# A transformer block on one core: first loads on two queues, bias product behind the first projections, and a new written order

## The chip, the cores and the metric

The kernel runs on one core of a Trainium2 chip. The core has five engines that work side by side: TensorE (PE, matrix products; its weight loads are listed apart as PEld), VectorE (DVE), ScalarE (ACT), GpSimd (POOL) and SyncE (SP, which here only issues DMAs). Each takes its instructions from its own queue, in the queue's order; they wait for one another by semaphores. The metric is the device time in microseconds (us) of one launch. Before the change the median of three runs is 478.84 us (478.42 to 479.89). About 0.3%, which is 1.4 us, is what a measurement of this kernel can tell from no change.

## What is computed

The input is 16 batches of 512 tokens with 256 features, in float32. The reference, cut to what matters:

```python
q, k, v = (heads(x @ W.T + b) for W, b in (Wq, bq), (Wk, bk), (Wv, bv))   # 16 heads of 16
qk_, kk_ = exp(q - max(q, -1)), exp(k - max(k, -1))
kv    = einsum('bhsd,bhse->bhde', kk_, v)
denom = einsum('bhqd,bhd->bhq', qk_, sum(kk_, 2)) + 1e-6
y     = einsum('bhqd,bhde->bhqe', qk_, kv) / denom[..., None]
x1  = layernorm(x + merge(y) @ Wo.T + bo)
h   = relu(x1 @ T(W1).T + b1)            # 1024 wide; T(W) = clip(round(W / (mean|W| + 1e-5)), -1, 1)
out = layernorm(x1 + h @ T(W2).T + b2)
```

Attention is linear: no product of tokens with tokens is formed. The two weight matrices of the feed-forward part become ternary.

## The kernel before

**Steps and the written order.** The whole program is a list of named steps. Some run once (`startup_steps`, L469 to L636: loading the weights, splitting them, making them ternary); the others run for each batch (`steps(b)`, L642 to L1230). A step is one instruction or a few on one engine: `qk3` of batch 1, for instance, is the six products that make q and k of the fourth 128 tokens of batch 1. A table `ORDER` (L103 on) gives each step a position, one number for each batch; the loop at the end (L1240 to L1251) emits the steps by these numbers and ties every instruction to the one ahead of it on its engine. So the table *is* the queue of each engine, across batches: several batches are under way at a time, and what stands first in a queue is waited for by all that stands behind it. No scheduler changes that order.

A second table, `OTHER` (L53 on), names for some steps the batches in which they run on the other of two engines. `engine()` (L407) reads it. Subtracting the maxima (`mxs`, L748), for example, is a POOL step unless the batch is listed, and then it is a DVE step; copying the upper half of the hidden values (`hc`, L1180/1182) is ACT's unless listed, and then DVE's.

**Precision.** A float32 operand is split into an upper part rounded to a faster format (a copy on ACT) and a lower part, the rest (a subtraction on DVE or POOL); a product is then three products (`TERMS`). Batch 0 goes without for q and k: its products (`qkF`, L718) use the loaded weights and tokens as they are, in plain float32, in two passes each.

**The stages of a batch.** Tokens transposed come from memory (`ldt`, L660, SP's queue; batch 0 in two halves a and b of each of two feature chunks 0 and 1), are split (`xt` L675, `xtl` L679), and multiplied with the weights of q and k (`qk` L728, or `qkF` L718). The bias is added (`mxa` L738, DVE), the maximum of each head found (`mxb` L744, DVE) and subtracted (`mxs` L748), and the exponential taken (`ex` L759/761, ACT). Sums over tokens (`ks` L782/784, `ksh` L789, `ksl` L793, product `pks` L806) give the denominators (`dena` L810, `denb` L825, `denc` L830, all DVE), and q is divided by them (`nrm` L838). In parallel the tokens, loaded again untransposed (`ldx`, L688), are multiplied with k (`g` L861, `gF` L857), then with the weights of v (`kv` L888), masked (`kvm`, `kvp`, `kvh`, `kvl`, L894 to L909) and multiplied with those of the output (`m` L916). Turned q (`qt` steps, L946 to L1012; `qtbl` is the lower part, L981) times m gives the attention's output (`o` L1134). The residual and the sum (`or`, `zr`, L1040, DVE), means, squares and variances (`nm`/`nq`/`nv`, `ym`/`yq`/`yv`, L1053 to L1086) and the scaling (`na`, `ya`, L1099 to L1105) are the two layer norms; `xb` (L871) and `x1b` (L1149) add biases ahead of them. Between them come eight hidden products for each batch (`f` L1168), their relu (`ha` L1174, ACT), upper and lower parts (`hc`, `hb` L1186, DVE), and eight products back (`z` L1205). `st` (L1224) stores.

**Accumulators.** PSUM, where products land, is divided into four tags of two banks each: one for q, k and transposes (`pbqk` uses it too), one for hidden products (`ph`; batch 0 also puts qkF2 and qkF3 there), one for the results `z` (and warm-up products), one for the rest. A product that needs a bank waits until the bank's last user has been read.

**The start.** `warm0` (L486) issues nine products of ones with ones, whose result nobody reads, and `warm1` two more much later (`WARM`, L51). `lqk0` and `lqk1` (L491 to L499) load the upper and the lower 128 rows of the weights of q and of k, four DMAs of 128 KB, all from ACT's queue. ACT then makes a tiny copy, for which it loads its table. `wh` and `wl` split these weights for the later batches. `lbqk` (L517) loads the two biases into row 0 of a tile that is zero elsewhere, and `pbqk` (L522) multiplies that tile with ones, so that the biases stand in all 128 rows; `bqke` (L526, ACT) copies them out of PSUM, and `mxa` adds them.

```python
                for j, w in enumerate((wqT, wkT)):
                    nc.scalar.dma_start(out=loaded[c][:, j * E:(j + 1) * E],
                                        in_=w[c * P:(c + 1) * P, :])
                if len(loaded) == EC:
                    nc.scalar.copy(tab, ones[:, 0:1])
```

TensorE's order at the start is: nine warm-up products, `pbqk`, `qkF0_0`, `qkF0_1` (first 128 tokens, feature chunks 0 and 1), `qkF1_0` and so on to `qkF3_1`, then `qk3` of batch 1, `warm1`, `tot0` (the sum for the ternary scale), `qk2` of batch 1, `pks` of batch 0, `gF`. SP's queue before starts with the two biases, then `ldt0a`, the tokens of batch 1, `ldt1a`, and pieces of the feed-forward weights among them. From `f0` of batch 0 on, hidden products and the next batches' q and k take turns.

Of the kernel before, what the change touches and what calls it, by code (L numbers as in the profile page):

```python
# [25 lines left out]
P = 128  # L26
# [24 lines left out]
WARM = (9, 2)  # L51
GROUPS = {"s": 2, ("y", 15): 4, ("s", 15): 4}
OTHER = {  # L53
    "mxs0": (0, 1, 6),
    "wol": (0,),
    "ks": (0, 1, 5, 8, 9, 10, 12, 15),
    "ksl": (0, 1, 2, 5, 6, 7, 9, 11, 12, 14, 15),
    "bvm": (0,),
    "kvp": (0, 3, 4, 5, 7, 9, 10, 12, 13, 15),
    "kvl": (0, 1, 3, 4, 6, 7, 8, 9, 10, 11, 12, 13, 15),  # L60
    "nrm0": (0, 7, 11, 13, 14),
    "xb0": (0, 2, 4, 5, 10, 11, 13),
    "xb1": (0, 3, 6, 10),
    "nm0": (0, 1, 2, 3, 5, 6, 10, 11, 14),
    "qc0": (0,),
    "qc2": (0,),
    "na2": (0, 3, 4, 8, 11, 12),
    "x1b1": (0, 13),
    "mxs3": (2, 6, 10, 11, 13),
    "nrm1": (2, 7, 8, 9, 10, 14),  # L70
    "ek0": (2, 3, 4, 5, 9, 10, 11, 13, 14, 15),
    "nv0": (1, 2, 4, 5, 7, 9, 10, 12, 13, 15),
    "x1b0": (0, 3, 8, 12),
    "hc1": (0, 4, 5, 6, 8, 14),
    "na0": (1, 6, 11, 13, 14, 15),
    "ek1": (3, 4, 6, 7, 8, 10, 11, 12),
    "xsl0": (3, 4, 11, 13),
    "xt1bl0": (1, 2, 4, 5, 9, 10, 13, 14),
    "hc2": (1, 6, 7, 9, 12, 14),
    "xtl1": (5, 8, 11, 12, 14),  # L80
    "hc0": (1, 3, 4, 9, 10, 11),
    "na3": (2, 4, 5, 10, 11, 15),
    "ya2": (0, 1, 5),
    "xsl1": (4, 9),
    "qtbl0": (3, 5, 7, 11, 13),
    "xtl0": (6,),
    "ym0": (1, 5, 6, 8, 9, 10, 11),
    "mxs1": (5, 7, 10, 15),
    "hc4": (2, 10, 14),
    "yv0": (1, 3, 7, 8),  # L90
    "hc5": (2, 6, 8, 9, 12, 15),
    "ya1": (1, 10, 11, 12, 13, 14),
    "qtbl1": (4, 7, 14, 15),
    "xt1bl1": (4, 5, 10, 12, 13, 14),
    "ya3": (3, 5, 11, 12, 13, 14),
    "na1": (6, 7, 14),
    "ya0": (4, 6, 8, 13, 14),
    "hc3": (7, 15),
    "hc6": (7, 12, 14, 15),
    "hc7": (9, 14),  # L100
    "yv1": (15,),
}
ORDER = {  # L103
    "lqk0": (0,),
    "lqk1": (1,),
    "wh0": (2,),
    "warm0": (3,),
    "lbqk": (4,),
    "wh1": (5,),
    "wl1": (6,),  # L110
    "ldt0a": (7, 0, 0, 0, 0, 0, 0, 0, 0, 0, 0, 0, 0, 0, 0, 0),
    "wl0": (8,),
    "pbqk": (9,),
    "bqke": (10,),
    "ldt1": (0, 11, 72, 132, 281, 334, 349, 553, 535, 734, 909, 1095, 1250, 1398, 1534, 1728),
    "ldt1a": (12, 0, 0, 0, 0, 0, 0, 0, 0, 0, 0, 0, 0, 0, 0, 0),
    "xt1": (0, 13, 74, 151, 282, 342, 499, 669, 767, 803, 1027, 1181, 1275, 1415, 1684, 1768),
    "xtl1": (0, 14, 90, 202, 317, 426, 528, 687, 834, 960, 1045, 1266, 1295, 1449, 1736, 1769),
    "ldt0": (0, 15, 81, 128, 204, 178, 416, 612, 703, 758, 864, 1194, 1272, 1410, 1492, 1511),
    "qkF0_0": (16, 0, 0, 0, 0, 0, 0, 0, 0, 0, 0, 0, 0, 0, 0, 0),  # L120
    "xt0": (0, 17, 82, 129, 297, 356, 505, 694, 779, 826, 1115, 1195, 1399, 1411, 1541, 1796),
    "xtl0": (0, 18, 91, 164, 298, 395, 515, 695, 832, 827, 1116, 1255, 1413, 1442, 1567, 1798),
    "qkF0_1": (19, 0, 0, 0, 0, 0, 0, 0, 0, 0, 0, 0, 0, 0, 0, 0),
    "mxa0": (20, 124, 189, 318, 344, 566, 654, 751, 989, 1166, 1223, 1338, 1463, 1611, 1824, 2057),
    "mxb0": (21, 126, 215, 319, 354, 592, 671, 761, 990, 1170, 1284, 1339, 1476, 1641, 1825, 2075),
    "qkF1_0": (22, 0, 0, 0, 0, 0, 0, 0, 0, 0, 0, 0, 0, 0, 0, 0),
    "mxs0": (23, 127, 233, 320, 425, 594, 672, 816, 1034, 1178, 1285, 1436, 1478, 1688, 1854, 2093),
    "qkF1_1": (24, 0, 0, 0, 0, 0, 0, 0, 0, 0, 0, 0, 0, 0, 0, 0),
    "lw1_0": (25,),
    "mxa1": (26, 98, 184, 235, 358, 485, 653, 743, 882, 1068, 1235, 1432, 1484, 1699, 1862, 1893),  # L130
    "mxb1": (27, 112, 221, 238, 360, 487, 661, 797, 899, 1129, 1236, 1433, 1485, 1718, 1872, 1962),
    "lwo": (28,),
    "woh": (29,),
    "wol": (30,),
    "ldt0b": (31, 0, 0, 0, 0, 0, 0, 0, 0, 0, 0, 0, 0, 0, 0, 0),
    "lw0_0": (32,),
    "sa0_0": (33,),
    "sg0_0": (34,),
    "exF0": (35, 141, 0, 0, 0, 0, 0, 0, 0, 0, 0, 0, 0, 0, 0, 0),
    "ldt1b": (36, 0, 0, 0, 0, 0, 0, 0, 0, 0, 0, 0, 0, 0, 0, 0),  # L140
    "qkF2_0": (37, 0, 0, 0, 0, 0, 0, 0, 0, 0, 0, 0, 0, 0, 0, 0),
    "qkF2_1": (38, 0, 0, 0, 0, 0, 0, 0, 0, 0, 0, 0, 0, 0, 0, 0),
    "qkF3_0": (39, 0, 0, 0, 0, 0, 0, 0, 0, 0, 0, 0, 0, 0, 0, 0),
    "mxa2": (40, 80, 175, 237, 440, 568, 623, 840, 945, 1035, 1292, 1312, 1571, 1661, 1802, 1990),
    "mxb2": (41, 121, 187, 289, 441, 569, 650, 842, 992, 1052, 1314, 1361, 1572, 1662, 1804, 1991),
    "lw0_2": (42,),
    "sa0_2": (43,),
    "lw0_1": (44,),
    "sa0_1": (45,),
    "qkF3_1": (46, 0, 0, 0, 0, 0, 0, 0, 0, 0, 0, 0, 0, 0, 0, 0),  # L150
    "mxa3": (47, 63, 222, 299, 389, 608, 730, 770, 922, 1064, 1202, 1359, 1532, 1664, 1751, 2004),
    "mxb3": (48, 71, 223, 307, 411, 609, 731, 777, 996, 1096, 1203, 1386, 1565, 1705, 1842, 2008),
    "mxs1": (49, 125, 225, 276, 486, 580, 686, 867, 916, 1152, 1276, 1444, 1488, 1719, 1873, 2058),
    "exF1": (50, 140, 0, 0, 0, 0, 0, 0, 0, 0, 0, 0, 0, 0, 0, 0),
    "lbo": (51,),
    "lw0_3": (52,),
    "lw1_3": (53,),
    "sa0_3": (54,),
    "sr0": (55,),
    "mxs2": (56, 122, 203, 290, 474, 578, 685, 892, 1024, 1136, 1317, 1382, 1573, 1673, 1814, 2028),  # L160
    "ldx": (57, 162, 145, 186, 418, 546, 670, 886, 934, 1107, 1335, 1401, 1568, 1619, 1764, 1972),
    "lbv": (58,),
    "sa1_0": (59,),
    "mxs3": (60, 111, 230, 326, 483, 621, 741, 820, 1022, 1145, 1282, 1456, 1570, 1716, 1895, 2070),
    "sg0_3": (61,),
    "qk3": (0, 62, 211, 262, 388, 577, 715, 766, 889, 1055, 1161, 1331, 1480, 1606, 1737, 1994),
    "lw1_1": (64,),
    "warm1": (65,),
    "tot0": (66,),
    "qk2": (0, 67, 155, 236, 392, 457, 593, 774, 884, 1018, 1190, 1302, 1495, 1634, 1793, 1915),  # L170
    "half0": (68,),
    "exF2": (69, 139, 0, 0, 0, 0, 0, 0, 0, 0, 0, 0, 0, 0, 0, 0),
    "exF3": (70, 120, 0, 0, 0, 0, 0, 0, 0, 0, 0, 0, 0, 0, 0, 0),
    "qz0": (73,),
    "ks": (75, 142, 248, 369, 502, 626, 762, 905, 1067, 1186, 1333, 1477, 1590, 1752, 1912, 2095),
    "ksh": (76, 148, 254, 370, 506, 632, 763, 917, 1075, 1192, 1371, 1481, 1600, 1753, 1913, 2119),
    "gF0": (77, 163, 0, 0, 0, 0, 0, 0, 0, 0, 0, 0, 0, 0, 0, 0),
    "qz3": (78,),
    "sg0_2": (79,),
    "sg1_0": (83,),  # L180
    "qz2": (84,),
    "ksl": (85, 149, 255, 378, 507, 633, 765, 918, 1082, 1193, 1372, 1482, 1605, 1765, 1936, 2127),
    "pks": (86, 160, 256, 390, 523, 699, 782, 941, 1106, 1217, 1387, 1497, 1620, 1777, 1937, 2136),
    "dena": (87, 161, 257, 391, 524, 700, 784, 950, 1117, 1227, 1390, 1498, 1621, 1778, 1940, 2137),
    "bvm": (88,),
    "kvb": (89, 196, 329, 406, 549, 717, 788, 987, 1150, 1218, 1427, 1506, 1632, 1783, 1945, 2159),
    "denb": (92, 177, 263, 394, 525, 701, 793, 951, 1118, 1228, 1391, 1500, 1622, 1780, 1941, 2138),
    "denc": (93, 179, 264, 398, 532, 702, 794, 952, 1119, 1240, 1404, 1525, 1638, 1792, 1942, 2139),
    "sa1_1": (94,),
    "gF1": (95, 170, 0, 0, 0, 0, 0, 0, 0, 0, 0, 0, 0, 0, 0, 0),  # L190
    "ge": (96, 171, 293, 424, 557, 668, 809, 962, 1163, 1279, 1425, 1569, 1675, 1781, 1971, 2142),
    "qk1": (0, 97, 183, 224, 357, 452, 618, 714, 862, 1046, 1234, 1403, 1457, 1695, 1819, 1892),
    "lwv": (99,),
    "kv": (100, 194, 310, 432, 562, 712, 825, 974, 1175, 1297, 1448, 1574, 1697, 1809, 1974, 2163),
    "kvm": (101, 200, 328, 433, 563, 724, 829, 976, 1177, 1298, 1462, 1582, 1706, 1810, 1975, 2169),
    "lw1_2": (102,),
    "sa1_2": (103,),
    "sg1_2": (104,),
    "lb2": (105,),
    "qk0": (0, 106, 188, 296, 337, 565, 643, 749, 968, 1165, 1206, 1316, 1452, 1610, 1800, 2037),  # L200
    "sa1_3": (107,),
    "sr1": (108,),
    "lb1": (109,),
# [185 lines left out]
def block_kernel(ctx: ExitStack, tc: tile.TileContext, x, xT, wqT, wkT, wvT, woT,  # L389
                 bq, bk, bv, bo, w1T, b1, w2T, b2, out):  # L390
    nc = tc.nc
    NB, S, E = x.shape
# [73 lines left out]
    loaded = {}  # L466
# [830 lines left out]
```

## Time and profile before

| quantity | before |
|---|---|
| median of 3 runs | 478.84 us (478.42 to 479.89) |
| profiled execution, its own time | 478.84 us |
| its span in the trace | 477.1 us |
| PE busy | 465.9 us (98%), 2964 products |
| PE weight loads, beside PE | 395.5 us (83%) |
| DVE busy | 435.0 us (91%), 855 instructions |
| ACT busy | 398.8 us (84%), 914 instructions |
| POOL busy | 369.4 us (77%), 382 instructions |
| DMA | 58.53 MB, 123 GB/s on average |

The profiled execution's own time is the median, and 1.74 us of it lie outside the span. Busy shares are averages over the whole span, over stages with different limits. A view by windows gives the busy time of each engine in a stretch of the span; the view of waits gives, for each engine, the instruction that it waited for; the timeline gives instructions in order of time, with the idle time ahead of them and what ended it in brackets.

### The profile page before, as it was taken

The page shows a single profiled execution, that of the slowest core. Times are in us where ns is not written, and L with a number is a line of the kernel's source. Part 1 is how long each engine was busy: PE and PEld are TensorE (multiplying, and loading weights), DVE is VectorE, ACT ScalarE, POOL GpSimd, SP SyncE. Part 2 cuts the span into 40 slices and gives each one's busy share as a digit, 9 for nine tenths or more (in the row PEclk, how much of TensorE's full clock was granted, in tenths as well). Part 3 has the DMA queues.
Part 4 walks back from the last instruction along what each step waited for, and adds up shares of the span by engine and source line. Part 5 has one row for each costly group of instructions (what it writes and reads, how often), then busy time and mean ns, then how long its engine had stood idle before and what let it go on. Part 6 is the DMA issues. An engine that isn't in the chain of part 4 may idle for free. (4 is left out here: it accounts for less than half of the span.)

```text
span 477.1 us, 8950 instructions
## 1 busy us (share of the span) xinstructions
PE 465.9 (98%) x2964; PEld 395.5 (83%) x2964; DVE 435.0 (91%) x855; ACT 398.8 (84%) x914; POOL 369.4 (77%) x382
## 2 busy tenths in 40 slices
PE   9999999999999999999999999999999999999994
PEld 5777888797897888889888887978888898988874
DVE  4999899999999999999999999899999799988965
ACT  4996787897969889999969899987987988988873
POOL 4679887988888979798698989989889866436432
PEclk9999999999999999999999999999999999999999
DMA  8921035261533462433544525343441154123102
GB/s 254 340 69 45 1 125 162 77 211 68 155 110 99 145 197 94 152 113 111 176 111 133 174 94 166 123 132 112 137 162 58 42 200 137 64 89 133 45 1 89
DMA packets 35667, 58.53 MB, mean 123 GB/s; under 512 B 4130, under 2 KB 21796, under 8 KB 35620
## 3 DMA queue, kind: packets, MB, share of 16 engines
q1 hardware_dynamic: 35044, 57.43, 36.8%
q10 hardware_dynamic: 576, 0.52, 0.4%
q8 instruction: 23, 0.38, 0.4%
q14 instruction: 24, 0.20, 0.1%
HBM read 34.87 MB, written 23.07 MB: 121 GB/s over the span
## 5 line engine op out<-in xcount | busy, mean ns | idle before, releaser
L1174 ACT ACTIVATE ph<-ph,b_sb 128x512 f32<-128x512 f32 x128 | 83.7, 655 | 21.5 <-PE ph L1168 20.8
L748 POOL TENSOR_TENSOR qk<-qk,mx 128x512 f32<-128x512 f32 x52 | 57.4, 1111 | 8.4 <-DVE mx L744 7.7
L759 ACT ACTIVATE ex<-qk 128x512 f32<-128x512 f32 x64 | 39.9, 626 | 10.3 <-POOL qk L748 7.5
L738 DVE TENSOR_TENSOR qk<-pqk,bqk 128x512 f32<-128x512 f32 x64 | 43.3, 680 | 2.6 <-ACT xt_1h L675 1.0
L744 DVE TENSOR_REDUCE mx<-qk 128x32 f32<-128x512 f32 x64 | 43.2, 678 | 0.9
L1149 POOL TENSOR_TENSOR x1b<-x,b_bc 128x512 f32<-128x512 f32 x26 | 34.2, 1319 | 1.5 <-ACT x L1103 1.4
L1065 ACT ACTIVATE junk_z<-x1b,nm_z 128x256 f32<-128x256 f32 x62 | 31.1, 503 | 3.5 <-POOL nm_z L1055 3.0
L1065 ACT ACTIVATE junk_o<-x,nm_o 128x256 f32<-128x256 f32 x64 | 32.0, 502 | 2.4 <-POOL nm_o L1055 2.1
L1168 PEld LDWEIGHTS <-w1f 128*128 128x128 f16 x256 | 15.7, 98 | 19.7 <-issue 16.5
L871 POOL TENSOR_TENSOR x<-x,bo_bc 128x512 f32<-128x512 f32 x21 | 29.8, 1419 | 0.6
L838 POOL TENSOR_TENSOR qs<-ex,rden 128x512 f32<-128x512 f32 x21 | 24.3, 1170 | 7.2 <-DVE rden L830 7.1
L1103 ACT ACTIVATE x<-x,nmr_o,rstd_o 128x256 f32<-128x256 f32 x43 | 24.3, 597 | 4.5 <-POOL nmr_o L1086 4.5
L1040 DVE SCALAR_TENSOR_TENSOR x<-po,x 128x256 f32<-128x256 f32 x64 | 24.5, 417 | 2.4 <-PE po L1134 1.5
L1103 ACT ACTIVATE x1b<-x1b,nmr_z,rstd_z 128x256 f32<-128x256 f32 x41 | 23.3, 597 | 3.8 <-POOL nmr_z L1086 3.7
L1040 DVE SCALAR_TENSOR_TENSOR x1b<-pz,x1b 128x256 f32<-128x256 f32 x62 | 23.4, 414 | 1.7 <-PE pz L1205 1.5
L1084 POOL TENSOR_TENSOR rstd_o<-var_o,expo 128x4 f32<-128x4 f32 x16 | 17.6, 1101 | 7.7 <-ACT var_o L1078 7.3
L825 DVE TENSOR_REDUCE den<-dent 128x64 f32<-128x1088 f32 x16 | 20.5, 1284 | 0.4
L1084 POOL TENSOR_TENSOR rstd_z<-var_z,expo 128x4 f32<-128x4 f32 (+1 forms) x19 | 19.0, 998 | 1.5 <-ACT var_z L1078 0.9
L946 DVE STREAM_TRANSPOSE rqT<-qs 128x1024 f32<-128x1024 f32 x14 | 17.4, 1241 | 2.2 <-POOL qT_10l L981 1.2
L810 DVE TENSOR_TENSOR dent<-ex,pks 128x1024 f32<-128x1024 f32 x16 | 19.3, 1208 | 0.0
L946 DVE STREAM_TRANSPOSE rx1T<-x 128x1024 f32<-128x1024 f32 x14 | 17.4, 1242 | 1.3 <-ACT x L1103 0.7
L888 PEld LDWEIGHTS pkv<-g,wv 128*128 128x128 f32 x128 | 16.2, 191 | 0.9 <-ACT g L880 0.2
(877 smaller groups left out, 2038.0 us busy)
## 6 DMA issues: line engine op xcount, KB each, us to landing
x<-in_x_dram SPq DMA_DIRECT2D x16, 512.0 KB, 4.5
xt<-in_xT_dram SPq DMA_DIRECT2D x30, 256.0 KB, 3.8
out_dram<-x1b SPq DMA_DIRECT2D x30, 256.0 KB, 2.2
wqT<-rqT SPq DMA_DIRECT2D x14, 512.0 KB, 2.9
dqT<-wqT SPq DMA_DIRECT2D x56, 128.0 KB, 2.9
wx1T<-rx1T SPq DMA_DIRECT2D x14, 512.0 KB, 2.9
dx1T<-wx1T SPq DMA_DIRECT2D x56, 128.0 KB, 3.1
w<-in_w2T_dram SPq DMA_DIRECT2D x4, 256.0 KB, 5.2
```

The costliest lines, as they stand in the source:

```text
L738: nc.vector.tensor_tensor(s.qk[t].rearrange("p g d -> p (g d)"), s.pqk[t], bqk, ALU.add)
L744: nc.vector.tensor_reduce(s.mx[t], s.qk[t], AX.X, ALU.max)
L748: engine(f"mxs{t}", b, nc.gpsimd, nc.vector).tensor_tensor(s.qk[t], s.qk[t], s.mx[t].unsqueeze(2).to_broadcast([P, 2 * NH, HD]), ALU.subtract)
L759: nc.scalar.activation(s.ex[:, t, :], qk, AF.Exp)
L871: engine(f"xb{h}", b, nc.gpsimd, nc.vector).tensor_tensor(r, r, bo_bc.unsqueeze(1).to_broadcast([P, 2, E]), ALU.add)
L946: nc.vector.transpose(pts["r"].rearrange("p (j y w) -> p j y w", j=P // SQ, w=SQ), getattr(s, src).rearrange("p t (c j v) -> p j (t c) v", ...
L1040: nc.vector.scalar_tensor_tensor(out=r, in0=p[t], scalar=1.0, in1=r, op0=ALU.mult, op1=ALU.add, accum_out=stat("sum")[:, t:t + 1])
L1065: nc.scalar.activation(junk, getattr(s, what)[:, t, :], AF.Square, bias=n.nm[:, t:t + 1], accum_out=stat("sq")[:, t:t + 1])
L1084: nc.gpsimd.tensor_tensor(stat("rstd")[:, sl], n.var[:, sl], expo[:, sl], ALU.pow)
L1103: nc.scalar.activation(r, r, AF.Identity, bias=nmr, scale=rstd)
L1149: engine(f"x1b{h}", b, nc.gpsimd, nc.vector).tensor_tensor(s.x1b[:, tt, :], s.x32[:, tt, :], b2_bc.unsqueeze(1).to_broadcast([P, 2, E]), A ...
L1174: nc.scalar.activation(s.ph[f], s.ph[f], AF.Relu, bias=b1_sb[:, f:f + 1])
```

## The change

Four edits.

The loads of the weights of q stay on ACT's queue; those of k go to SP's. The second warm-up step issues one product where it issued two. Both tables are written anew, so that the order of steps on every engine changes throughout the program, and so does the engine of many steps. At the start, the first tokens of batch 0 (`ldt0a`, `ldt1a`) now stand in front of all other loads of SP's queue, with the two halves of k's weights between and behind them, the biases next, then batch 1's tokens; and `pbqk` and `bqke` stand behind `qkF0_0` and `qkF0_1`. TensorE then goes on with `qkF2_0`, `qkF1_0`, `qkF1_1`, `qkF2_1`, `qkF3_0`, `qkF3_1`, `qk3` of batch 1, `tot0`, `qk2`, `gF0`, `pks`.

In `OTHER`, the net count of steps for each engine moves like this. DVE gains `hc` (5), `qtbl` (7), `kvl` (4), `mxs` (3), `nrm` (3), `xtl` (3), `xb` (1) and `x1b` (1), and gives up `ek` (2), `ks` (1), `ksl` (3), `xsl` (1) and `ya` (5). POOL has 19 steps fewer, ACT 4 more. SP issues the two loads of k's weights in addition.

The diff, cut to the edit of the code, the lines of the start, and some of the steps named in the prediction:

```diff
-WARM = (9, 2)
+WARM = (9, 1)
...
-    "mxs0": (0, 1, 6),
+    "mxs1": (1, 3, 10, 12, 13, 15),
+    "mxs0": (1, 2, 9, 14),
+    "mxs2": (6, 13),
+    "mxs3": (6, 9, 10),
-    "mxs3": (2, 6, 10, 11, 13),
-    "mxs1": (5, 7, 10, 15),
-    "qtbl0": (3, 5, 7, 11, 13),
-    "qtbl1": (4, 7, 14, 15),
+    "qtbl1": (2, 3, 6, 7, 10, 12, 13, 14, 15),
+    "qtbl0": (3, 6, 7, 9, 10, 12, 15),
...
-    "lqk0": (0,),
-    "lqk1": (1,),
-    "wh0": (2,),
-    "warm0": (3,),
+    "ldt0a": (0, 0, 0, 0, 0, 0, 0, 0, 0, 0, 0, 0, 0, 0, 0, 0),
+    "lqk0": (1,),
+    "ldt1a": (2, 0, 0, 0, 0, 0, 0, 0, 0, 0, 0, 0, 0, 0, 0, 0),
+    "lqk1": (3,),
     "lbqk": (4,),
-    "ldt0a": (7, 0, 0, 0, 0, 0, 0, 0, 0, 0, 0, 0, 0, 0, 0, 0),
-    "pbqk": (9,),
-    "bqke": (10,),
-    "ldt1a": (12, 0, 0, 0, 0, 0, 0, 0, 0, 0, 0, 0, 0, 0, 0, 0),
-    "qkF0_0": (16, 0, 0, 0, 0, 0, 0, 0, 0, 0, 0, 0, 0, 0, 0, 0),
-    "qkF0_1": (19, 0, 0, 0, 0, 0, 0, 0, 0, 0, 0, 0, 0, 0, 0, 0),
-    "mxa0": (20, 124, 189, 318, 344, 566, 654, 751, 989, 1166, 1223, 1338, 1463, 1611, 1824, 2057),
+    "wh0": (5,),
+    "warm0": (6,),
+    "qkF0_0": (11, 0, 0, 0, 0, 0, 0, 0, 0, 0, 0, 0, 0, 0, 0, 0),
+    "qkF0_1": (14, 0, 0, 0, 0, 0, 0, 0, 0, 0, 0, 0, 0, 0, 0, 0),
+    "pbqk": (15,),
+    "ldt0b": (16, 0, 0, 0, 0, 0, 0, 0, 0, 0, 0, 0, 0, 0, 0, 0),
+    "qkF2_0": (17, 0, 0, 0, 0, 0, 0, 0, 0, 0, 0, 0, 0, 0, 0, 0),
+    "bqke": (18,),
+    "mxa0": (24, 130, 173, 340, 376, 561, 651, 761, 950, 1167, 1191, 1350, 1457, 1579, 1809, 2042),
-    "warm1": (65,),
...
-                for j, w in enumerate((wqT, wkT)):
-                    nc.scalar.dma_start(out=loaded[c][:, j * E:(j + 1) * E],
-                                        in_=w[c * P:(c + 1) * P, :])
+                for j, (w, queue) in enumerate(((wqT, nc.scalar), (wkT, nc.sync))):
+                    queue.dma_start(out=loaded[c][:, j * E:(j + 1) * E],
+                                    in_=w[c * P:(c + 1) * P, :])
```

The two loads of `lqk0` thus go out one on each queue, and those of `lqk1` likewise. In the changed file every line behind the tables stands three lines further down.

## The prediction

> **What bounds the kernel now.** I read the page's busy times first, then the windows, the waits of PE, and the timeline of the first and last 20 us.
>
> ```profile
> span 477.1 us, 8950 instructions
> PE 465.9 (98%) x2964; PEld 395.5 (83%) x2964; DVE 435.0 (91%) x855; ACT 398.8 (84%) x914; POOL 369.4 (77%) x382
> ```
>
> PE is the bound, and DVE is close behind. From the windows (columns: us; busy us of PE, PEld, DVE, ACT, POOL; granted clock; DMA share; GB/s):
>
> ```profile
> 0.00:20.00 20.00, 18.88 (x63) 12.16 (x63) 12.53 (x25) 12.85 (x28) 9.54 (x17) 1.00 0.89 290
> 20.00:40.00 20.00, 19.06 (x95) 15.91 (x96) 19.48 (x36) 16.91 (x41) 16.21 (x17) 1.00 0.30 106
> 80.00:100.00 20.00, 20.00 (x122) 16.26 (x121) 19.47 (x36) 17.88 (x43) 18.47 (x21) 1.00 0.26 94
> 340.00:360.00 20.00, 18.77 (x116) 15.81 (x115) 19.20 (x35) 18.21 (x41) 17.38 (x17) 1.00 0.42 132
> ```
>
> The first 20 us belong to DMA (share 0.89), the next to DVE (19.48 against PE's 19.06), the middle to PE with DVE close enough to take over in bursts. The waits of PE, in us:
>
> ```profile
> PE ph L1168 <- DVE h_1l L1186: 1.7, 2, 1.2
> PE po L1134 <- DVE m_10l L931: 0.6, 1, 0.6
> PE pqT L989 <- DVE qs L838: 0.5, 1, 0.5
> PE pks L806 <- POOL ksd_0l L793: 0.4, 1, 0.4
> ```
>
> In the middle it is nearly always DVE that PE waits for. To count this, I added up PE's products at the interval from one issue to the next where nothing is waited for: 458.0 us. PE's place in time less the work done by then is 1.4 us at `qk3` of batch 1 (13.9 us), 5.5 at `f0` of batch 0 (45.5) and 12.5 at `f0` of batch 15 (454.8). So of the 12.5 us lost, 1.1 go before PE can start, about 4.1 between 14 and 45 us, and 7.0 in the middle. Longer waits in the middle, as such gaps, sum to 3.9 us (1.38 and 0.60 for h_1l, 0.78 for m_10l, 0.48 for POOL's ksd, 0.34 for `mxa`, 0.32 for h_2l).
>
> **The start, up to the first accumulator.** From the timeline:
>
> ```profile
> 1.10 4.21 PE L486 MATMUL pwarm<-ones 128*128 128x128 f32 x18 [1.10 <-DVE ones L447]
> 5.10 1.92 PE L522 MATMUL pbqk<-bqk,ones 128*128 128x512 f32 x2
> 6.81 3.77 PE L718 MATMUL pqk<-w32qk,xt 128*128 128x512 f32 x8
> 7.05 0.59 ACT L526 COPY bqk<-pbqk 128x512 f32<-128x512 f32 x1 [0.45 <-PE pbqk L522]
> 8.96 0.69 DVE L738 TENSOR_TENSOR qk<-pqk,bqk 128x512 f32<-128x512 f32 x1 [1.03 <-ACT xt_1h L675]
> ```
>
> Warm-up products hold PE until 5.10 in both kernels, so data that land earlier than that gain nothing. Then come three steps: the bias's two passes at half clock (0.85 each, to 6.81), and `qkF0_0` (0.60 + 0.43) and `qkF0_1` (0.43 + 0.43) to 8.70. After the change the same three steps stand in the order `qkF0_0`, `qkF0_1`, bias: whichever is first pays the half clock, and all are done at 5.10 + 1.71 + 1.03 + 0.86 = 8.70 again. Condition: the half token tile and q's and k's upper rows (384 KB) by 5.10 and the next 384 KB by 6.81. Before, 384 KB had landed by 3.79 and 512 KB by 5.91; SP's first DMA was issued at 1.62 behind a memset of the bias tile, and now needn't wait for that. I take no stall (bounds 0 to 0.8).
>
> The split of queues itself removes two issues from ACT (0.45 each) and adds two on SP; ACT's table load starts earlier, and both lie beside the warm-ups. PE waits for none of them: 0.
>
> What does come later is the bias: its copy ends at about 9.5 instead of 7.64, so `mxa0` starts near 9.6 instead of 8.96, +0.6 for DVE. PE covers this, as `qkF2_0` and `qkF1_0` have banks of their own (the latter takes `pbqk`'s). POOL's chain (`mxs`, 1.11 each by the page) then brings the last exponential to about 18.0 and `ks` to 18.05, which was 17.98; `pks` follows at 20.4, as before. The second warm-up product dropped is two passes of 0.11: −0.2.
>
> The granted clock is 0.5 until 7.16 in this trace, 6.06 us after the first product. [...]
>
> **20 to 46 us.** DVE has no gap to speak of from 14.6 to 47.8, and PE waits for it. From `dena` of batch 0 (20.96) to the second lower part of x1T (ends 45.28) before takes 24.32. The steps that the changed order puts in DVE's queue between these two, each at the median of its row, sum to 24.45; with the idle time that the old stretch has (24.32 less 23.45 busy, 0.9) and a subtraction that DVE did in 1.21 there, not in its mean of 0.81, 46.4 is the changed end, against 45.28. That is +1.2 (bounds: 0, if no idle remains, and +2.0 with the late bias's 0.6 and a late `qs` like the one in the waits on top).
>
> **The middle.** The costs of the engine moves, by DVE's rows:
>
> | moved to DVE | each us | sum |
> |---|---|---|
> | hc +5 (L1182) | .68 | 3.4 |
> | qtbl +7 (L981) | .9 | 6.3 |
> | mxs +3 (L748) | .81 | 2.4 |
> | nrm +3 (L838) | .83 | 2.5 |
> | xtl +3 (L679) | 1.0 | 3.0 |
> | kvl +4, xb +1, x1b +1 | .43, .85, .71 | 3.3 |
> | off: ek 2, ks 1, ksl 3, xsl 1, ya 5 | .73, 1.28, .76, 1.0, .46 | −8.4 |
>
> The sum is +12.5 us for DVE: 435.0 to about 447 of 477, 94%. (`kvl`'s rows on DVE, L909, lie at .41 to .44, those of `qtbl` at .68 to 1.35.) By the same sum over rows POOL loses some 18 us and ACT gains 1.5, and neither is the bound. On average DVE still fits. What matters is where it doesn't: I summed DVE's and PE's rows along both written orders, in pieces of 20 us of PE's work. In the old order one pair of neighbours exceeds PE: 300 to 340, DVE 44.4 against PE 41.1, excess 3.3, and there the loss grew by 3.2 (8.9 to 12.1). In the new order that pair falls to 41.5 against 39.6 (excess 1.9), but three more arise: 60 to 80 (21.6 against 20.1, 1.5), 160 to 180 (23.4 against 19.9, 3.5), 220 to 240 (22.7 against 19.9, 2.8). Together 9.7. Each has neighbours in which DVE has 2 to 4 us to spare, where before had its excess twice running. If none costs anything, before's 3.3 is gained: −3.3. If all do, 9.7 − 3.3 = +6.4. I take half, 4.85 − 3.3 = **+1.5**.
>
> **The tail.** The last `z7`, its residual, statistics, scaling and store are on the same engines in the same order; the last batch's one mean that changes engine (`ym1` to ACT) and its variance (`yv1` to POOL) are single instructions of 0.2: 0 (±0.3).
>
> **The sum**, against the profiled execution's own 478.84 us, which is also the median: 478.84 − 0.2 + 0 + 1.2 + 1.5 + 0 = **481.3 us**.
>
> [...] DMA's share is 0.81 to 1.10 of its engines from 2 to 23 us, so more queues find no free engine. [...]
>
> **The rivals.**
>
> *Faster (the other side).* The middle's bursts fall into slack: 16 batches interleave, the orders have cushions of several us between DVE's steps and PE's, and the old order's bad pair is halved. Then the middle gives −3.3 and the start only the late bias's 0.6: 478.84 − 0.2 + 0.6 − 3.3 = 475.9. It decides if PE's waits for DVE behind 60 us sum to less than 1.5 us. For it: the long waits of before are six, and none need recur. Against: DVE at 94%.
>
> *No change.* The new bursts cost what the old pair did, and idle time in DVE's first 45 us goes: 478.84 − 0.2 + 0.2 = 478.8.
>
> *The bursts cost in full.* +6.4 in the middle and +2.0 at the start: 478.84 − 0.2 + 2.0 + 6.4 = 487.0. Against it: the trace's windows before 300 us hold DVE at 19.5 of 20 with PE at 20.00 (80 to 100).
>
> *The change doesn't do what it says.* The early tokens bring nothing at PE, as reckoned above. This is in the forecast already; only if the first products wait for k's weights, now behind the first tokens on SP's queue, does it cost, up to the 0.8.
>
> **How the numbers follow.** Forecast, 480.3 to 486.0: 0.50. In full, above 486: 0.05. No change, 477.4 to 480.3: 0.17. Faster: 0.28, about a third of it below 475.5. A measurement of this kernel tells about 0.3% (1.4 us) from no change. So slower 0.55, same 0.17, faster 0.28. The range 475.5 to 486.0 leaves out 0.05 and 0.10, and takes in most of the bounds of the middle; forecasts of both signs being likely, the forecast's own range is 480.3 to 486.0.
>
> **What would show it.** In the changed profile: `qkF0_0` at 5.1 and three steps done at 8.7; `mxa0` near 9.6; the second lower part of x1T at 46.4, where PE's loss is 7 us and not 5.5; DVE busy near 447; windows near 165 to 185 and 225 to 245 with PE below 20.00 and DVE above 19.5. It is wrong if PE begins `qkF0_0` late for loads, if `f0` comes at or before 45.5, or if PE's loss in the middle is below 7.0.

## The result and the profile after

The changed kernel takes 480.44 us (median of ten runs, 479.75 to 481.19) against 478.75 us for the kernel before in the same job: a ratio of 1.0035, 95% interval 1.0025 to 1.0044, so 1.7 us more (1.2 to 2.1). The forecast was 481.3 us, in a range from 480.3 to 486.0.

The page after, its first lines:

```profile
span 478.6 us, 8946 instructions
PE 465.2 (97%) x2962; PEld 394.4 (82%) x2962; DVE 443.0 (93%) x869; ACT 400.4 (84%) x918; POOL 351.8 (73%) x364
```

DVE has 8.0 us more to do and POOL 17.6 less; PE is as busy as it was. The windows after (columns as in the prediction), the four shown there and the one in which most is lost:

```profile
0.00:20.00 20.00, 17.35 (x59) 11.03 (x59) 12.17 (x24) 12.72 (x27) 9.05 (x17) 1.00 0.87 288
20.00:40.00 20.00, 19.51 (x95) 15.80 (x96) 19.79 (x40) 17.29 (x41) 13.42 (x13) 1.00 0.35 121
60.00:80.00 20.00, 17.93 (x117) 15.48 (x116) 19.84 (x27) 13.97 (x29) 16.82 (x14) 1.00 0.42 130
80.00:100.00 20.00, 19.82 (x122) 16.27 (x121) 18.84 (x42) 17.61 (x43) 17.34 (x20) 1.00 0.32 109
340.00:360.00 20.00, 20.00 (x131) 16.80 (x130) 19.18 (x35) 18.26 (x41) 17.38 (x19) 1.00 0.41 126
```

From 60 to 80 us PE has lost 2 us beside a DVE that is busy all the time but has finished only 27 instructions, where in the other windows behind 20 us it finished 35 to 42; four of the 27 took much longer than their kind does elsewhere (two of them are named below). From 340 to 360, where the kernel before lost 1.2, nothing is lost. The waits of PE after:

```profile
PE ph L1171 <- DVE h_5l L1189: 2.2, 2, 1.2
...
PE pqk L721 <- DMA xt<-in_xT_dram: 1.1, 1, 1.1
PE pz L1208 <- DVE h_7l L1189: 1.1, 1, 1.1
PE ph L1171 <- DVE h_4l L1189: 0.6, 1, 0.6
```

Before's long waits are gone or smaller (the product behind m_10l still waits, 0.37 us at 316.54 and not 0.78), and others of the same kind are there. As the gap over PE's usual issue interval they are 1.24 us at 11.48 (tokens), 1.16 at 65.73 (h_5l), 1.23 at 78.88 (h_7l), 1.41 at 245.0 (h_5l) and 0.73 at 378.69 (h_4l). Behind the first hidden product each kernel has six gaps of more than 0.3 us; they sum to 3.9 us in before and 5.2 in after. PE's loss, counted as in the prediction, is 5.56 us at the first hidden product of batch 0 (before 5.51), and 14.41 at that of batch 15 (before 12.48). So between these two places the change costs 1.9 us, and ahead of them nothing in these two profiles, in which the full clock came at different moments (4.88 us in after, 7.16 in before).

What the slow stretch is made of shows in the timeline of PE, DVE and POOL, 76 to 79 us:

```profile
78.88 0.39 PE L1208 MATMUL pz<-w,h_7l 128*128 128x256 f32 x1 [1.07 <-DVE h_7l L1189]
```

```profile
76.46 1.76 DVE L984 TENSOR_TENSOR qT_2l<-dqT,qT_2h 128x512 fp32r<-128x512 f32 x1
78.15 0.68 DVE L1189 TENSOR_TENSOR h_7l<-ph,h_7h 128x512 fp32r<-128x512 f32 x1
```

```profile
76.38 1.29 POOL L984 TENSOR_TENSOR qT_2l<-dqT,qT_2h 128x512 fp32r<-128x512 f32 x1
77.63 1.73 POOL L785 TENSOR_TENSOR ks<-ex 128x512 f32<-128x512 f32 x1
```

DVE's first line is a subtraction that takes 0.68 us in most places. Here it takes 1.76: it ends 0.55 us after POOL's instruction that began 0.08 earlier. `h_7l`, for which PE waits, stands behind it. POOL's next takes 1.73 in its turn instead of 1.29. In before 22 DVE instructions are stretched by over 0.25 us, in after 21. Each of them reads only from SBUF and begins while a POOL instruction is under way, or within 20 ns of its start; each ends 0.15 to 0.55 us after POOL's has. The converse holds too: of DVE's additions, subtractions and products of two operands in SBUF, none that began with no POOL instruction under way, or only one of 4 columns, is stretched (68 in before, 92 in after). The four long waits of after stand behind such instructions: `qz7` (1.85, usually 0.74), `qtbl1` of batch 2 (1.76), `kvp` of batch 8 (1.13, usually 0.42) with `ya3` of batch 5 (0.89, usually 0.40), and `na2` of batch 12 (1.17, usually 0.40). `qtbl1` and `kvp` have two inputs, `ya3` and `na2` are `tensor_scalar` with one tensor: both kinds are stretched. By what means POOL's instruction does it no run shows.

### The profile page after: what moved, and what is told of

Same layout as the page of the kernel before. It is cut to its first block, busy times and chain, and to the rows that moved or that the text cites. A ratio compares the mean times of both kernels' runs of the same rounds, so it can differ in the third digit from the quotient of the medians.

```text
span 478.6 us, 8946 instructions
## 1 busy us (share of the span) xinstructions
PE 465.2 (97%) x2962; PEld 394.4 (82%) x2962; DVE 443.0 (93%) x869; ACT 400.4 (84%) x918; POOL 351.8 (73%) x364
## 5 line engine op out<-in xcount | busy, mean ns | idle before, releaser
L751 POOL TENSOR_TENSOR qk<-qk,mx 128x512 f32<-128x512 f32 x49 | 56.0, 1147 | 14.6 <-DVE mx L747 8.1
L1152 POOL TENSOR_TENSOR x1b<-x,b_bc 128x512 f32<-128x512 f32 x25 | 33.0, 1326 | 2.1 <-DMA out_dram<-x1b 1.8
L1106 ACT ACTIVATE x1b<-x1b,nmr_z,rstd_z 128x256 f32<-128x256 f32 x46 | 25.0, 595 | 3.4 <-POOL nmr_z L1089 3.3
L874 POOL TENSOR_TENSOR x<-x,bo_bc 128x512 f32<-128x512 f32 x20 | 26.7, 1339 | 0.8 <-PE pg L860 0.8
L841 POOL TENSOR_TENSOR qs<-ex,rden 128x512 f32<-128x512 f32 x18 | 22.3, 1244 | 6.1 <-DVE rden L833 5.8
L1106 ACT ACTIVATE x<-x,nmr_o,rstd_o 128x256 f32<-128x256 f32 x43 | 23.2, 593 | 3.1 <-POOL nmr_o L1089 3.0
L1043 DVE SCALAR_TENSOR_TENSOR x1b<-pz,x1b 128x256 f32<-128x256 f32 x62 | 23.5, 416 | 1.8 <-PE pz L1208 1.7
L1087 POOL TENSOR_TENSOR rstd_o<-var_o,expo 128x4 f32<-128x4 f32 x16 | 16.5, 1031 | 2.5 <-ACT var_o L1081 1.8
```

Of the source, the lines that this page charges most:

```text
L751: engine(f"mxs{t}", b, nc.gpsimd, nc.vector).tensor_tensor(s.qk[t], s.qk[t], s.mx[t].unsqueeze(2).to_broadcast([P, 2 * NH, HD]), ALU.subtract)
L874: engine(f"xb{h}", b, nc.gpsimd, nc.vector).tensor_tensor(r, r, bo_bc.unsqueeze(1).to_broadcast([P, 2, E]), ALU.add)
L1043: nc.vector.scalar_tensor_tensor(out=r, in0=p[t], scalar=1.0, in1=r, op0=ALU.mult, op1=ALU.add, accum_out=stat("sum")[:, t:t + 1])
L1087: nc.gpsimd.tensor_tensor(stat("rstd")[:, sl], n.var[:, sl], expo[:, sl], ALU.pow)
L1106: nc.scalar.activation(r, r, AF.Identity, bias=nmr, scale=rstd)
L1152: engine(f"x1b{h}", b, nc.gpsimd, nc.vector).tensor_tensor(s.x1b[:, tt, :], s.x32[:, tt, :], b2_bc.unsqueeze(1).to_broadcast([P, 2, E]), A ...
```

## The experiments

Each kernel was measured beside the kernel before, whose median in the three jobs was 478.45, 478.28 and 478.76 us. Code is shown in outline. Where a kernel has the same products as another, the text also compares when PE starts the same product in the two profiles: that shows where time is won or lost, and whether it stays so.

**Start and rest exchanged (start_new, start_old).** The cut is at `f0` of batch 0: one kernel takes the changed steps up to there and the old ones behind it, the other the converse. The tables were written as

```diff
+sequence = after[:after.index(("f0", 0))]            # or before[...]
+sequence += [s for s in before if s not in sequence]  # or after
```

> The changed start alone: code of the change (queues, one warm-up product, early tokens, late bias) and all its steps up to f0 of batch 0, with their engines; every later step in the old order on its old engine. In the two traces the loss of PE is 5.51 us (before) and 5.56 us (after) at that point, so the theory that the new later order costs the time expects the kernel before less 0.2, within 0.5: 478.1 to 479.1. The rival, that the start costs it (my 1.2 us there, which an earlier clock in the one profile of after may hide: full from 4.88 us against 7.16), expects 479.6 to 480.4.

> The converse: old code and old steps up to f0 of batch 0, then every other step in the new order on its new engine. If the later order costs it, all of the change's cost is here: 480.2 to 481.0, with PE waiting for h_5l, h_7l, h_5l and h_4l as in after. If the start costs it, 478.6 to 479.4.

Measured: start_new 481.74 us (1.0083, 1.0065 to 1.0100), start_old 481.68 (1.0076, 1.0061 to 1.0091). Both are slower than either parent, which neither theory had. The trace tells why: the cut itself makes a wait. Steps that one order puts ahead of the cut and the other behind it meet at the seam, and in start_new PE waits there longest:

```profile
PE pks L807 <- DVE x L1041: 2.7, 2, 2.5
PE ph L1169 <- DVE h_1l L1187: 1.7, 2, 1.2
```

The gap at 57.9 us is 2.70 and one at 50.87 is 0.40; behind them the waits are those of before (0.61, 0.39, 0.78, 0.48, 1.38). In start_old a gap of 1.08 stands at 48.81, behind it are those of after (1.22, 1.23, 1.41, 0.73). Less the seams, that is 478.6 and 480.6, which would put the cost into the later order. But this is a subtraction, not a measurement, so the cut was moved.

**The head alone (head_new, head_old).** The cut is where the two orders differ by three steps, behind the first 22 of the changed order: the queues, the early tokens, the late bias, the warm-up (and one split of batch 1's tokens, `xtl1`, on its new engine).

> The four named parts of the change and nothing else: the two queues, early tokens, the bias behind the first products (the changed order's first 22 steps, up to the last split of batch 1's tokens) and one warm-up product less; then the old order with the old engines. My forecast's head (0, and 0.6 for the late bias in part covered): the kernel before -0.2 to +0.4, 478.2 to 478.9. The rival that the early tokens pay: 477.5 or less. The rival that the late bias is passed on to the end: 479.0 or more.

> The converse: old code and the old order's first 20 steps (loads of q and k all on ScalarE's queue, bias product in front), then the changed order with its engines. If the head is neutral, the changed kernel's time, 480.2 to 480.8. If the new head gained and the new order lost more, 481.0 or more; if the new head lost, 479.9 or less.

Measured: head_new 478.94 us (1.0015, 1.0004 to 1.0027), so 0.7 us more than before (0.2 to 1.3); head_old 480.46 us (1.0050, 1.0033 to 1.0067), the changed kernel's own 480.44. The head gains nothing, and in the old order it seems to cost a little. head_new lies between the forecast's upper end (478.9) and the late bias's lower (479.0) and decides between neither; that early tokens pay is out. Part of the 0.7 can be chance: ten of before's 23 runs in this job lie at 477.1 to 477.7, a group apart from the rest (see one_step). The profile of head_new shows what became of the early start. PE in order of time:

```profile
5.11 1.88 PE L718 MATMUL pqk<-w32qk,xt 128*128 128x512 f32 x4
6.83 1.02 PE L522 MATMUL pbqk<-bqk,ones 128*128 128x512 f32 x2
7.68 2.82 PE L718 MATMUL pqk<-w32qk,xt 128*128 128x512 f32 x6
12.15 1.13 PE L718 MATMUL pqk<-w32qk,xt 128*128 128x512 f32 x2 [1.64 <-DMA xt<-in_xT_dram]
```

The three steps that the prediction had done at 8.70 are done at 7.68, because the clock was granted in full from 5.10 (7.16 in the profile of before); and then PE stands for 1.64 us until the second halves of the tokens land. In one_step, further down, which has the old head, the clock came at 3.97 and PE waited 2.0 us in all for tokens. Product by product, head_new's PE is 0.5 us behind before's at 13 us and 0.4 at the end: what is lost for the tokens stays lost. Whichever of these heads it is, products that start earlier meet the loads.

**The first third exchanged (third_new, third_old).** The other place where the orders have nearly the same steps behind them, three of 731 apart, lies at about 178 us.

> The changed order with its engines up to the place where both orders have all but a few of the same steps behind them (731 of the changed order, about 178 us), then the old one. By the two traces PE's loss there is 9.48 us (after) and 7.75 (before), at the start of q and k of batch 8: if the waits of the first third are the cost, 480.0 to 480.6. The rival, that the cost is spread over the whole program by 12.5 us more work on VectorE, expects a third of it: 478.8 to 479.2.

> The converse: old order up to that place, the changed one behind it. If the first third carries the cost: 478.5 to 479.0 (the loss behind it is 4.93 us in after and 4.73 in before). If it is spread with VectorE's work: 479.5 to 480.1.

Measured: third_new 479.32 us (1.0025, 1.0014 to 1.0036), third_old 479.69 (1.0037, 1.0023 to 1.0051). third_new lies in neither expected range, third_old in that of the rival, the spread cost. But in third_old a seam cost again what the first third should have saved: gaps of 0.73, 0.42 and 0.37 at 157.7, 159.7 and 179.8, which neither parent has; so its agreement says little. third_new has no such seam. Its PE begins the hidden products 0.7 us ahead of before's (44.8 against 45.5) and is 1.46 us behind at 180, with after's waits in between (1.19 at 65.21, 1.23 at 78.36), and still 1.35 behind at 345. So the changed order does lose its time in this third. The total is less because of what comes then. The last two thirds are before's order step for step, but the longest wait there, 1.38 us at 346.82 in before, has shrunk to 0.28. DVE and POOL in before around it:

```profile
343.01 1.78 DVE L679 TENSOR_TENSOR xt_14l<-xt,xt_14h 128x512 fp32r<-128x512 f32 x1
```

```profile
342.96 1.27 POOL L767 TENSOR_TENSOR exk_13l<-ex,exk_13h 128x512 fp32r<-128x512 f32 x1 [0.32 <-ACT exk_13h L761]
```

and the same two instructions in third_new, whose lines are three further down:

```profile
344.34 0.69 DVE L682 TENSOR_TENSOR xt_14l<-xt,xt_14h 128x512 fp32r<-128x512 f32 x1
```

```profile
344.31 1.88 POOL L770 TENSOR_TENSOR exk_13l<-ex,exk_13h 128x512 fp32r<-128x512 f32 x1 [0.33 <-ACT exk_13h L764]
```

In before they begin 50 ns apart and DVE's is the one that takes longer (1.78 against 0.69); in third_new 30 ns apart, and it is POOL's (1.88 against 1.27). Nothing in the order around them differs. PE's wait differs by 1.1 us with which of the two is held up, and PE keeps the difference to the end. The recorded starts don't tell which it will be: POOL's is the earlier in both.

**One step moved (one_step).** So that step was moved out of the encounter: `xtl1` of batch 14 ahead of `na3` of batch 11, for which DVE stood idle 0.59 us anyway.

```diff
-... ("na3", 11), ..., ("xtl1", 14), ("qk3", 14)
+... ("xtl1", 14), ("na3", 11), ..., ("qk3", 14)
```

> The kernel before with one VectorE step one place further forward: xtl1 of batch 14 stands ahead of na3 of batch 11. In before's trace xtl1 began at 343.01, 50 ns behind a subtraction of GpSimd (ek0 of batch 13), took 1.78 us and not 0.68, and PE waited 1.38 us for h_1l at 346.82; in third_new the same pair began 30 ns apart, xtl1 took 0.69, GpSimd's took 1.88 instead of 1.27, and the wait was 0.28. Theory A (the wait is this coincidence): without it about 1.1 to 1.4 us less, and the kernel before's runs, which fall into 477.1 to 477.5 and 478.3 to 479.3, have a counterpart in the lower group alone: median 477.0 to 477.5. Rival B (the wait is VectorE's load in that stretch): VectorE does the same work, so 478.0 to 478.7 as before.

Measured: 477.45 us (0.9970, 0.9956 to 0.9984), 1.4 us less than before, with DVE's work unchanged (434.5 us busy, 435.0 before). The moved step takes its usual time:

```profile
342.65 0.68 DVE L679 TENSOR_TENSOR xt_14l<-xt,xt_14h 128x512 fp32r<-128x512 f32 x1
```

PE is 0.65 us behind before's up to 345 (it waited for tokens at the start), and 0.7 ahead from 348 to the end: the 1.38 are won at this one place. Its twelve runs lie between 476.99 and 478.15 in one group; those of before beside them lie in two, three at 477.5 to 477.6 and the others from 478.5 on. The median is in theory A's range. That before's two groups are the two outcomes of this encounter fits, but no profile of before from the lower group was taken, so it is not shown.

**Four long waits of after (four_off, locks_off).** The first takes the stretched instructions away from DVE or behind the one that PE waits for; the second leaves DVE's work and takes POOL's partner away. (It leaves out four differences, so four lower parts hold copies and the result is not the reference's: it is a test, not a kernel to use.)

```diff
-"qtbl1": (2, 3, 6, ...)      # four_off: qtbl1 of batch 2 to POOL, kvp of batch 8 to POOL
-"ya3": (0, 1, 5, ...)        # ya3 of batch 5 and na2 of batch 12 to ACT; qz7 behind hb5 of batch 0
+if (key, c, b) in (("qt", 0, 2), ("qt", 0, 13)):   # locks_off; the same for ksl and xsl1 of batch 9
+    nc.scalar.copy(laid_out(lo), pts["d"][:, c])
```

> The change, with four VectorE instructions taken away from ahead of the four long waits of PE (1.16, 1.23, 1.41 and 0.73 us): one ternary weight piece (qz7) goes behind hb5 of batch 0, qtbl1 of batch 2 and kvp of batch 8 go to GpSimd, ya3 of batch 5 and na2 of batch 12 to ScalarE. Together they took 1.85 + 1.76 + 1.13 + 0.89 + 1.17 = 6.8 us there, of which 3.9 is more than such instructions take elsewhere. If the four waits are lost time and nothing else is late next, 480.4 - 4.5 = 475.9, below both kernels; if the waits only move to the next step of VectorE's queue, 479 to 480.5.

> The change, with VectorE's work as it is, but four subtractions of GpSimd that ran beside three of the stretched instructions taken from GpSimd: qtbl0 of batches 2 and 13, xsl1 of batch 9 and ksl of batch 9 are copies on ScalarE instead of differences, so these lower parts hold other values. Theory A: VectorE's instructions are stretched because GpSimd runs at the same moment; without it qtbl1 of batch 2 takes 0.7 and not 1.76, kvp of batch 8 0.4 and not 1.13, ya3 of batch 5 0.4 and not 0.89, na2 of batch 12 0.4 and not 1.17, and the waits behind them (1.23, 1.41, 0.73) shrink to 0.2 or less: 477.4 to 478.5. Rival B: it is the amount of work moved to VectorE that makes PE late; that is unchanged here, so 480.0 to 480.9.

Measured: four_off 479.86 us (1.0035, 1.0021 to 1.0050 against before), locks_off 483.39 (1.0112, 1.0090 to 1.0134). In four_off the gaps at 65.73 and 378.69 are gone, but 0.77 us for `qtbl1`, now POOL's, and 0.69 for POOL's `ksl` stand at 78 and 82, and four gaps from 0.39 to 0.79 at 243 to 246, where there was one of 1.41. The time is in the rival's range, and by the ratios no better than after's (1.0035 both). But not every wait only moved. Product by product, four_off's PE runs level with after's up to 64 us, is 1.15 us ahead from 68 and still 1.07 ahead at 240; it then loses 1.3 at 243 to 246, and wins 0.7 at 378.7, of which 0.4 is left at the end. The waits behind `qz7` and `na2` were lost time; what ate the gain stands at 245. In locks_off all four instructions are short:

```profile
76.64 0.68 DVE L993 TENSOR_TENSOR qT_2l<-dqT,qT_2h 128x512 fp32r<-128x512 f32 x1
77.24 0.68 DVE L1198 TENSOR_TENSOR h_7l<-ph,h_7h 128x512 fp32r<-128x512 f32 x1
```

`qtbl1` takes 0.68 for 1.76 (`kvp` 0.42 for 1.13, `ya3` 0.41 for 0.89, `na2` 0.40 for 1.17), and PE's wait of 1.23 behind the first is gone: that DVE is stretched by POOL's instruction, and not slow of itself, is shown. It was lost time, too: PE, 0.18 us behind after's at 75, is 0.90 ahead at 80, and 0.94 ahead at 240, with as much for DVE to do as in after. The total is longer all the same, and outside both expected ranges. ACT had to take the copy of `qtbl0` of batch 13 in POOL's place, behind relus and copies of hidden values, and PE waited for it:

```profile
PE po L1146 <- ACT qT_13l L991: 2.8, 1, 2.8
```

PE goes from 0.6 us ahead at 375 to 4.4 behind at 390: the stop of 3.0 us, and products at half clock behind it. And at 244 PE still waited 1.25, though `kvp` and `ya3` were short, and 0.80 more at 245.6 for h_6l. DVE has `mxa0` of batch 10 between the two short instructions, and it could not start earlier:

```profile
239.37 0.69 DVE L744 TENSOR_TENSOR qk<-pqk,bqk 128x512 f32<-128x512 f32 x1 [0.67 <-issue]
```

```profile
237.84 0.60 ACT L704 CAST xs_9l<-x 128x512 fp32r<-128x512 f32 x1
238.88 0.40 ACT L767 ACTIVATE exk_9h<-qk 128x256 fp32r<-128x256 f32 x1
```

The view names no releaser ("issue"). `mxa0` begins 0.09 us after ACT's second line ends, and the trace has its last semaphore from that instruction (239.29), the one from PE 0.2 before it (239.08). ACT's first line is one of the copies added here. So the time won ahead of `mxa0` was not passed on.

**Order and engines exchanged (new_order, new_engines).** The forecast's reason was DVE's added work. So the changed order ran with the old table of engines, and the old order with the new table; nothing else differs.

```diff
-OTHER = after's        ORDER = after's
+OTHER = before's       ORDER = after's       # new_order; new_engines is the converse
```

> The change with its order, queues and warm-up, but each step on the engine that it had before: VectorE loses the 12.5 us that the change moved to it. If the load moved to VectorE costs the 1.7 to 1.9 us of the middle, as the forecast had it: 478.3 to 479.0. If it is coincidences in the new order, whoever does the work: 479.7 to 481.5.

> The converse: the old order, queues and warm-up, and each step on the engine that the change gives it; VectorE has about 12 us more to do than before, in the old order. If the load costs: 479.8 to 480.6. If the order costs, and the engines only shift where steps coincide: within 1 us of the kernel before, 477.3 to 479.3.

Measured: new_order 568.08 us (1.1859, 1.1831 to 1.1886), new_engines 586.14 (1.2243, 1.2220 to 1.2265). Some 90 and 107 us more, where no theory had more than 3. The page of new_order:

```profile
PE 495.5 (88%) x2962; PEld 408.6 (72%) x2962; DVE 457.7 (81%) x855; ACT 401.2 (71%) x914; POOL 369.0 (65%) x382
```

No engine is full. PE has 74 gaps of more than 0.25 us, 76.8 us in all (11 and 8.3 in after): 39 us for DVE's results, 22 for POOL's, 10 for ACT's. The longest is at 96.86, and can be followed. PE waits 4.50 us for DVE's residual; DVE, in the trace, for POOL:

```profile
94.27 0.08 DVE L1040 DVE_READ_ACCUMULATOR x1b<-pz,x1b 128x1 f32 x1
95.94 0.42 DVE L1040 SCALAR_TENSOR_TENSOR x<-po,x 128x256 f32<-128x256 f32 x1 [1.59 <-POOL x L871]
```

```profile
94.44 0.23 POOL L1055 TENSOR_SCALAR nm_z<-sum_z 128x4 f32<-128x4 f32 x1 [2.96 <-DVE x1b L1040]
94.64 1.27 POOL L871 TENSOR_TENSOR x<-x,bo_bc 128x512 f32<-128x512 f32 x1
```

The last line is `xb1` of batch 2. The change gives it to DVE at this place (position 373); the old table gives it to POOL, and in POOL's queue a mean stands just ahead of it (`ym0` of batch 0, position 369, which the change has on ACT), which waits 2.96 us for DVE's own residuals. PE's 4.50 us stand behind this step of 1.27. The two tables differ in 247 such assignments.

**A better kernel (five_steps).** The step of one_step, and three other waits of before taken away by order alone, each step on its engine:

```diff
+("ml", 10) ahead of ("qtr", 11)        # DVE idled 1.19 us for the transpose
+("hb1", 2) ahead of ("zr0", 1)
+("ksl", 12) ahead of ("ek1", 12)       # POOL
-WARM = (9, 2)
+WARM = (9, 1)
```

> The same, and three more waits of before taken away by order alone, every step on its old engine: ml of batch 10 ahead of a transpose for which VectorE idles 1.19 us (PE's wait 0.78), hb1 of batch 2 ahead of a residual (0.60), ksl of batch 12 ahead of ek1 on GpSimd (0.48); and one warm-up product for two (0.2). If waits taken away are time won: 477.2 - 0.78 - 0.35 - 0.48 - 0.2 = 475.4. If PE then meets the next step of VectorE's or GpSimd's queue: 476.2 to 477.2.

Measured: 476.88 us (0.9965, 0.9953 to 0.9977), 1.7 us less than before and, by the two ratios, 3.3 less than after; it is the second expectation that came. The gaps of 0.78 and 0.48 are gone and 0.60 is 0.26, but a new one of 0.64 stands at 323.8 (POOL's `kvl` of batch 11, behind the `ksl` moved forward), and the one at 152 grew from 0.34 to 0.62. Of the 1.6 us taken away at these places 0.9 came back there. Its median is 0.57 us below one_step's in the same job, and ten of one_step's twelve runs lie above its highest (477.12). But that is less than the 0.3% that a measurement can tell, and the two intervals overlap: that it is better than one_step is likely, and not shown.

## Why the prediction came out as it did

The forecast's sum was right to 0.9 us, with 480.44 just inside the range (its lower end is 480.3). It was so by errors that go against each other: the start's +1.2 did not come, and the middle's +1.5 was more.

*What bounds the kernel:* as forecast; PE's loss, not its work, makes the difference (base work 458.0 and 457.8 us, loss 12.5 and 14.4 at batch 15).

*The first accumulator, 0:* right as a sum, on another path. The profile of after has the three steps done at 7.58, not 8.70, and `mxa0` at 8.40, not 9.6, because the clock was granted from 4.88. What I bounded as a stall of 0 to 0.8 for the first two steps came later: the second half of the tokens, which `qkF2_1` needs as the seventh step, kept PE 1.08 us in after and 1.64 in head_new. I had checked the first 768 KB and not the next. What was said of a second queue stood: head_new, which has it, gains nothing (no run has the second queue alone).

*20 to 46 us, +1.2:* this term failed in size. The second lower part of x1T ends at 44.79, not 46.4, and PE's loss at the first hidden product is 5.56, not 7. From `dena` to there the new order takes 24.05 us, less than my sum of rows (24.45) before any idle time: DVE is busy for 23.5 of it and idle for 0.5, not 0.9. The long subtraction that I carried over did not recur, and I had misread it: the one of 1.21 us stands at 10.41, ahead of this stretch; the one in it took 1.08. `f0` came at 45.33, at or before the 45.5 that the prediction named as a sign of being wrong, and for this term it was one. Measured on its own, the head costs 0.7 us (0.2 to 1.3); over the whole of the start the two profiles differ by 0.05, the earlier clock of after (1.1 us at the third step) against its wait for tokens (1.24).

*The middle, +1.5:* it was 1.9, and this is the change's cost. The size was right, the mechanism was not. Of the four bursts in which DVE's rows exceeded PE's, 60 to 80 lost 2.55 (excess 1.5), 160 to 180 lost 0.13 (excess 3.5, the largest), 220 to 260 lost 2.0 (excess 2.8), 300 to 320 lost 0.5 (1.9). "Half of them cost" came out by luck of places. The window from 165 to 185 that was to show it has PE at 20.00; that from 225 to 245 has it at 18.75. What stands at the losses is a DVE instruction stretched by a POOL instruction, a little ahead of a product with no cushion; four of the five (all but `qtbl1`) were on DVE before the change as well. That the stretch makes the loss is shown at 78.9, where locks_off, with POOL's partner gone and DVE's work as it was, has PE 1.1 us earlier for the next 160 us, and in before by one_step, 1.4 us faster with DVE's work unchanged. At 65.7 four_off shows that the time goes with the stretched instruction, which it only puts further back; at 378.7 the wait is gone in four_off and in locks_off. At 245 it is argued only. new_order, with the moved work taken back from DVE, became 90 us slower, but by waits of its own: it says nothing on load. DVE's busy time rose by 8.0 us, not 12.5: means of rows that hold stretched instructions were too dear for the steps moved (three more `xtl` cost 0.5 and not 3.0, seven more `qtbl` 4.9 and not 6.3).

*The faster rival* (the old waits don't recur, the new bursts fall into slack) had its first half nearly right: of the six only one recurred, halved (0.78, now 0.37). *No change* and *in full* did not come. *That the change doesn't do what it says* was true of the head, as the forecast had it.

*What stays open:* what the wait at 245 would cost without its encounter, since both kernels that took it away lost more there by something else; how much the change costs against before's faster group of runs alone; and why the changed order's encounters fall at tighter places than the old order's, if they do: with six long waits in each, 5.2 us against 3.9, that may be chance. But it is not the chance of one execution: the waits at 65.7, 78.9, 245 and 378.7 come again, a little later, in the profiles of start_old and head_old.

## What to carry to other kernels

Where every engine's queue is written out, an order and its assignment of engines are one plan: exchange half of it, and steps stand behind others that wait for something later. On a kernel whose bound engine is 98% busy, look not at sums of load but at the instruction ahead of each wait, and ask why it took longer there than its row's usual time. Here such a wait could be removed by moving one step a few places, and the next one in line must be looked up before the gain is counted.

## What the runs showed of the hardware

The DVE instructions that POOL held up are recorded as busy, with a longer duration and not with idle time ahead of them: the one at 76.46 in after follows its predecessor without a gap. So the page's busy time hides it: 0.68 us of work shows as 1.76, and only the shape's other instructions tell. POOL's power of 4 columns (1.55 us, L1084 in one_step) did not hold up the subtraction beside it (0.68), nor did any other of its kind in before or after.

The moment at which the full clock was granted differs from profile to profile: 7.16 us in before, 5.10 in head_new, 4.88 in after and 3.97 in one_step, with the first product at 1.10 in each. In before a pass of 512 columns takes 0.85 us ahead of that moment (`pbqk`) and 0.43 behind it (`qkF`). In locks_off the clock went back to half in a stop: PE stopped for 3.0 us, up to 381.5, and the clock was at half from 380.8 to 387.7, which the window from 380 to 388 shows as 0.57:

```profile
380.00:388.00 8.00, 6.47 (x27) 5.88 (x28) 2.64 (x11) 1.75 (x4) 2.42 (x3) 0.57 0.40 131
```

In locks_off the stop was thus paid twice, as the stop and as the slow products behind it: between 375 and 390 PE lost 5.0 us on after. In new_order, with its 76.8 us of gaps, the mean granted clock over the span is 0.96.
